# Cross-attention of a transformer block with keys on partitions, planned together with the end of self-attention

## Chip, cores and metric

The kernel runs on one core of a Trainium2 chip. The metric is device time in microseconds (us) of one launch. Five engines work side by side, each through its own list of instructions in program order: TensorE (PE, with weight loads shown apart as PEld), VectorE (DVE), ScalarE (ACT), GpSimd (POOL) and SyncE (SP, which here issues nearly all DMAs). They wait for each other through semaphores.

## What is computed

A transformer block over x of shape (2, 1024, 256): self-attention with 16 heads of 64, cross-attention to a context of 77 tokens, a gated feed-forward part with GELU, each behind a normalisation with shift and scale from a condition vector, and then a second feed-forward part with ternary weights and activations rounded to 8 bits. Cut to what matters here:

```python
h1 = adaln(x, t, norm1_w, norm1_b)
x = mha(h1, h1, attn1_wq, attn1_wk, attn1_wv, attn1_wo, attn1_bo) + x
h2 = adaln(x, t, norm2_w, norm2_b)
x = mha(h2, context, attn2_wq, attn2_wk, attn2_wv, attn2_wo, attn2_bo) + x
h3 = adaln(x, t, norm3_w, norm3_b)
x = glu_ff(h3, ff_w1, ff_b1, ff_w2, ff_b2) + x

def mha(xq, ctx, wq, wk, wv, wo, bo):        # 16 heads of 64
    q, k, v = xq @ wq, ctx @ wk, ctx @ wv
    attn = softmax(q @ k.T / sqrt(64))       # per head
    return (attn @ v) @ wo + bo
```

## The kernel before

The 2048 tokens are 16 tiles of 128, eight per batch element (`TB = 8`, `NT = 16`); the residual stream `r_sb` stays in SBUF throughout. All matmuls up to the ternary part are fp32.

**Self-attention** runs over 32 units (`NU`): batch element, pair of heads, half of the 1024 queries. Each unit has eight blocks of 128 keys, two per slot, so four slots per unit (`SLOTS`) and 128 in all (`NS`). Keys lie on partitions, queries in the free dimension. A slot issues the scores of its two key blocks (L351, into the two banks of `two_banks`), the copy out of PSUM on ACT (L970), the running maximum on DVE (L367), and, seven slots behind (`LAG`), the shift by the maximum (L404, DVE; one block of eight on POOL, L399), the exponential (L408, ACT), the running sum (L415, POOL) and the product with the values (L423). The maximum over all keys goes through a transpose and folds on DVE (L372 to L389), a small DMA to DRAM and a broadcast back (L390, L391); ACT then copies it to PSUM (L395). The sums are made by a matmul with ones (L455), go to DRAM and back in a packed form, are inverted on DVE (L486) and come back as a broadcast (L482 to L489) for POOL's multiplication (L499). Projections, values and the way back to tokens (`back_to_tokens`, its residual add L338) are spread over the slots by hand (`pieces`, `inner`, `extras`).

**The end of self-attention.** Slots 128 to 139 work off what the last units still have to do. The sums of the last two units are made by `sums_by_ones` (L444), for the last unit one matmul pair per key block, and inverted without packing by `inverted` (four reciprocals, L496). Six half tiles of cross-attention scores are laid between (`tail`), and the projection of the last four heads comes in one piece (`po_last`).

**Cross-attention, prepared.** During self-attention `CrossPair` forms for each pair of heads G = wq k^T and U = v wo of the 77 context tokens, so that scores are h G and the output is p U. They go to DRAM and are loaded whole (`load_g`, `load_u`).

**Cross-attention, before.** Queries lie on partitions. For each tile of 128 queries and each half of the heads: scores (`cross_scores`, L769: four groups of 308 columns, heads times 77 keys, over two halves of the 256 features), maximum per head and subtraction on DVE (L784, L787), exponential (L796, ACT), sum and reciprocal on DVE (L801, L802), division on POOL (L803). Then ten transposes of 128x128 (`cross_turned`, L815), copies (L823, L824, L826), ten output matmuls with U (`cross_out`, L836) and the residual add (L848). The loop `for n in range(3, NT + 1)` runs scores of tile n and output of tile n - 1 alternately; the norms for the next parts (L155, L162) and the ternary weights (L1104 to L1149) hang in it at slots given by hand (`mid`, `after`).

**After that** come the feed-forward part and the ternary part, ordered by a planner (`Plan`): steps with an engine, a cost, predecessors, a rank and possibly a ring of buffers; `Plan.run` issues them in the order in which a list schedule with these costs would start them. The order on each engine is fixed then; the costs have no other meaning. The up matmuls are L1611, the down matmuls L1637, the ternary matmuls L1466 and L1513, their transposes L1454 and L1502.

PSUM is full in both kernels: two pairs of banks by `two_banks` (tag "s"), one bank "f" (`piece_bank`), one bank "av", and one pair "mb".

The loop over tiles, cut:

```python
for n in range(3, NT + 1):
    cross_scores(n, 0); cross_shifted(n, 0)
    cross_turned(n - 1, 0)
    cross_exp(n, 0); cross_divided(n, 0)
    cross_scores(n, 1); cross_shifted(n, 1)
    cross_turned(n - 1, 1)
    cross_exp(n, 1)
    po = cross_out(n - 1)
    cross_divided(n, 1)
    cross_added(n - 1, po)
```

## Time and profile before

| | us |
|---|---|
| median of 3 runs | 1192.07 (1191.5 to 1193.33) |
| profiled execution | 1191.9 |
| its span, first to last instruction | 1190.1 |
| first cross-attention scores on PE | 766.4 |
| feed-forward matmuls without a break from | 969.65 |

Times in the profile count from the start of the span. A row of the groups gives the source line, engine, operation, output and inputs, count, busy time and mean duration of one in ns, and the idle time of the engine just before with what ended it. A row of the stretches gives start and end, length, and then for PE, PEld, DVE, ACT and POOL the busy time with the number of instructions that start in it, the clock granted to PE as a share of the full one, and the share and rate of the DMAs. Rows in order of time give start, duration, engine, line, operation, and in brackets an idle time with its releaser. Matmuls are pipelined, so their durations overlap; from start to start is their pace. Every fp32 matmul of the code shows as two records.

### The profile page before, as it was taken

The page shows a single profiled execution, that of the slowest core. Times are in us where ns is not written, and L with a number is a line of the kernel's source. Part 1 is how long each engine was busy: PE and PEld are TensorE (multiplying, and loading weights), DVE is VectorE, ACT ScalarE, POOL GpSimd, SP SyncE. Part 2 cuts the span into 40 slices and gives each one's busy share as a digit, 9 for nine tenths or more (in the row PEclk, how much of TensorE's full clock was granted, in tenths as well). Part 3 has the DMA queues.
Part 4 walks back from the last instruction along what each step waited for, and adds up shares of the span by engine and source line. Part 5 has one row for each costly group of instructions (what it writes and reads, how often), then busy time and mean ns, then how long its engine had stood idle before and what let it go on. Part 6 is the DMA issues. An engine that isn't in the chain of part 4 may idle for free.

```text
span 1190.1 us, 16832 instructions
## 1 busy us (share of the span) xinstructions
PE 1153.1 (97%) x5972; PEld 565.8 (48%) x5980; DVE 947.2 (80%) x1397; ACT 810.3 (68%) x1034; POOL 811.4 (68%) x628
## 2 busy tenths in 40 slices
PE   8998999999999999999999999999999999999996
PEld 4332334333334343343333332346878856486684
DVE  5798889789889888998888988984767753578596
ACT  4788887888887887888789788651343441555366
POOL 5689888888888888889888998941425325423244
PEclk9999999999999999999999999999999999999996
DMA  7011211222121221211213112210020021000000
GB/s 236 32 32 50 80 46 60 73 61 66 50 79 47 70 71 48 77 41 60 65 45 123 37 46 90 90 54 36 1 83 5 1 63 36 1 18 10 9 10 27
DMA packets 66013, 63.24 MB, mean 53 GB/s; under 512 B 22935, under 2 KB 56329, under 8 KB 65417
## 3 DMA queue, kind: packets, MB, share of 16 engines
q1 hardware_dynamic: 65865, 62.15, 16.9%
q8 instruction: 47, 0.77, 0.3%
q14 instruction: 37, 0.30, 0.1%
q10 hardware_dynamic: 64, 0.02, 0.0%
HBM read 54.63 MB, written 7.52 MB: 52 GB/s over the span
## 4 chain that ended last, share of the span: by engine, by line
PE 80%; DVE 11%; ACT 4%; issue 2%; DMA 1%; POOL 1%; ACTq 0%; DVEq 0%; POOLq 0%; SPq 0%
PE sc L351 17%; PE pav L423 16%; PE pu L1611 9%; PE pp L285 8%; PE sc L769 5%; PE po L836 5%; PE pv L285 4%; PE po L1637 4%; DVE macc L367 4%; DVE sT L404 3%; PE po L285 3%; ACT sT L970 2%; PE tot L455 1%; PE pu L1466 1%; PE po L1513 1%
## 5 line engine op out<-in xcount | busy, mean ns | idle before, releaser
L415 POOL TENSOR_TENSOR pacc<-pacc,sT 128x1024 f32<-128x1024 f32 x186 | 441.4, 2373 | 47.2 <-ACT sT L408 37.2
L970 ACT COPY sT<-sc 128x1024 f32<-128x1024 f32 x256 | 247.8, 1015 | 54.9 <-PE sc L351 45.7
L367 DVE TENSOR_TENSOR macc<-macc,sc 128x1024 f32<-128x1024 f32 x192 | 233.7, 1217 | 63.7 <-ACT sT L970 52.0
L408 ACT ACTIVATE sT<-sT 128x1024 f32<-128x1024 f32 x256 | 259.9, 1062 | 16.1 <-DVE sT L404 14.8
L351 PE MATMUL sc<-qT,kT 64*128 64x512 f32 x1024 | 258.0, 619 | 6.5 <-DVE macc L367 5.8
L404 DVE TENSOR_TENSOR sT<-sT,mb 128x1024 f32<-128x1024 f32 x225 | 261.7, 1207 | 3.0 <-ACT mb L395 3.0
L423 PE MATMUL pav<-sT,v 128*64 128x512 f32 x1024 | 250.1, 606 | 5.3 <-ACT sT L408 4.9
L351 PEld LDWEIGHTS sc<-qT,kT 64*128 64x128 f32 x1024 | 85.7, 185 | 146.1 <-DVE macc L367 63.9
L423 PEld LDWEIGHTS pav<-sT,v 128*64 128x64 f32 x1024 | 62.3, 136 | 155.6 <-issue 76.8
L1611 PE MATMUL pu<-h2T,ffw 128*128 128x512 f32 (+1 forms) x320 | 114.6, 509 | 0.0
L803 POOL TENSOR_TENSOR pr<-pr,t 128x616 f32<-128x616 f32 x32 | 38.9, 1217 | 104.1 <-DVE t L802 59.9
L415 POOL TENSOR_TENSOR pacc<-sT 128x1024 f32<-128x1024 f32 x31 | 73.9, 2384 | 36.9 <-ACT sT L408 36.9
L1611 PEld LDWEIGHTS pu<-h2T,ffw 128*128 128x128 f32 x320 | 59.5, 190 | 44.0 <-issue 39.9
L769 PE MATMUL sc<-G,h1T 128*128 128x308 f32 x256 | 73.2, 429 | 4.5 <-DVE pr L787 3.6
L836 PE MATMUL po<-U,pT 128*128 128x256 f32 (+1 forms) x320 | 72.8, 381 | 3.9 <-ACT pT L826 2.4
L399 POOL TENSOR_TENSOR sT<-sT,wide 128x1024 f32<-128x1024 f32 x31 | 73.7, 2378 | 1.6 <-DMA wide<-md 1.6
L836 PEld LDWEIGHTS po<-U,pT 128*128 128x128 f32 (+1 forms) x320 | 59.3, 190 | 13.0 <-ACT pT L826 3.2
L285 PE MATMUL pp<-h1T,wk 128*64 128x512 f32 x256 | 60.6, 594 | 0.9 <-ACT h1T L561 0.9
L285 PE MATMUL pv<-wv,h1T 128*64 128x256 f32 x512 | 60.8, 379 | 0.0
L285 PE MATMUL pp<-h1T,wq 128*64 128x512 f32 x256 | 60.5, 593 | 0.0
L1629 DVE SCALAR_TENSOR_TENSOR gT<-pu,vecT,ge 128x512 f32<-128x512 f32 (+1 forms) x40 | 25.6, 641 | 42.0 <-ACT ge L1622 41.7
L769 PEld LDWEIGHTS sc<-G,h1T 128*128 128x128 f32 x256 | 46.9, 191 | 23.2 <-issue 6.2
(190 smaller groups left out, 1518.5 us busy)
## 6 DMA issues: line engine op xcount, KB each, us to landing
wide<-md SPq DMA_DIRECT2D x32, 512.0 KB
rinv<-td SPq DMA_DIRECT2D x60, 128.0 KB
ffw<-in_L_xcond_ff_w_dram SPq DMA_DIRECT2D x3, 1024.0 KB
gd<-cw SPq DMA_DIRECT2D x32, 77.0 KB
ud<-cw SPq DMA_DIRECT2D x32, 77.0 KB
G<-gd SPq DMA_DIRECT2D x2, 1232.0 KB
wk<-in_L_xcond_attn_wk_dram SPq DMA_DIRECT2D x16, 128.0 KB
wq<-in_L_xcond_attn_wq_dram SPq DMA_DIRECT2D x16, 128.0 KB
```

Source lines behind the costliest of these rows:

```text
L285: nc.tensor.matmul(dst[half, :], lhsT=lhsT[:, half], rhs=rhs, start=start, stop=stop)
L351: nc.tensor.matmul(sc[:, j * 512 : (j + 1) * 512], lhsT=kTs[b, pair][rows, kb * P : (kb + 1) * P], rhs=qTs[b, pair][rows, qh * 512 : (qh + ...
L367: nc.vector.tensor_tensor(maccs[u], old, sc, ALU.max)
L399: nc.gpsimd.tensor_tensor(t, t, wides[u], ALU.subtract)
L404: nc.vector.tensor_tensor(sT[u, kb], sT[u, kb], mbs[u], ALU.subtract)
L408: nc.scalar.activation(t, t, AF.Exp)
L415: nc.gpsimd.tensor_tensor(paccs[u], old, t, ALU.add)
L423: nc.tensor.matmul(pavs[u][j * DH : (j + 1) * DH, :], lhsT=vs[b, pair // 2][:, kb, at : at + DH], rhs=sT[u, kb][:, j * 512 : (j + 1) * 512 ...
L769: nc.tensor.matmul(sc[:, i * 512 : i * 512 + HB * CTX], lhsT=hT[:, c, qb * P : (qb + 1) * P], rhs=Gs[b][:, c, at : at + HB * CTX], start=( ...
L836: nc.tensor.matmul(po[:, :D], lhsT=pT2s[n, part][:w, i * P : (i + 1) * P], rhs=Us[b][:w, half * 5 + c, :], start=(half + c == 0), stop=(ha ...
L970: nc.scalar.copy(sT[v, kb], sc)
L1611: nc.tensor.matmul(pu[:, k * 512 : k * 512 + n], lhsT=ffw1[c][:, at : at + P], rhs=hT[:, c, at0 : at0 + n], start=(c == 0), stop=(c == DC ...
```

## The change

Cross-attention is turned round: keys on partitions, queries in the free dimension, in batches of 512 queries (four batches). The 77 keys become 80 (`KEYS`, three of them doubled), so that 16 heads times 80 keys make ten pieces of 128 rows: piece i holds keys i, i + 10, ... of each head, eight per head. The doubled keys are taken out of the softmax by a bias of -30000 on the last row of each head (`again`) in the three last pieces. A batch has five tiles of two pieces (1024 columns). The maximum over keys is taken over all pieces on DVE, turned by four transposes, folded per head, spread and turned back; the sums are made on POOL and go the same way. The output needs no transposes any more: the quotients stand as PE wants them.

```diff
+        KP = P // H
+        NPIECE = -(-CTX // KP)
+        KEYS = KP * NPIECE
+        TWICE = KEYS - CTX
-        HK = H * CTX
+        HK = H * KEYS
...
+        def load_g(b):
...
+            Gs[b] = [t.rearrange("p (x i) -> p i x", i=NPIECE) for t in halves]
+        def load_u(b):
+            Us[b] = gu.tile([P, GU], FP, tag="gu", name="U").rearrange("p (i d) -> p i d", d=D)
+            nc.sync.dma_start(out=Us[b], in_=ud[b].rearrange("(p i) d -> p i d", i=NPIECE))
...
+        class Batch:
+            def scores(self, k):
+                sc = self.sc[k] = two_banks("sc2")
+                hT = norms[1, self.b].hT
+                for j in range(2):
+                    for c in range(DC):
+                        nc.tensor.matmul(
+                            sc[:, j * 512 : (j + 1) * 512],
+                            lhsT=Gs[self.b][c][:, 2 * k + j, :],
+                            rhs=hT[:, c, self.at : self.at + 512],
+                            start=(c == 0), stop=(c == DC - 1),
+                        )
+                self.t[k] = p3.tile([P, 1024], FP, tag="sT", name="p2")
+            def kept(self, k):
+                nc.scalar.copy(self.t[k], self.sc[k])
+            def larger(self, k):
...
+                nc.vector.tensor_tensor(self.macc, old, self.sc[k], ALU.max)
+            def largest(self):
+                m = self.macc[:, :512]
+                nc.vector.tensor_tensor(m, m, self.macc[:, 512:], ALU.max)
+            def turned(self, bank, src=None):
+                for i in range(4):
+                    at = slice(i * P, (i + 1) * P)
+                    nc.tensor.transpose(bank[:, at], src[:, at], ident)
+            def folded(self, op):
+                nc.vector.tensor_reduce(
+                    few, self.bank.rearrange("p (x k) -> p x k", k=KP), AX.X, op
+                )
+                if op == ALU.add:
+                    nc.vector.reciprocal(few, few)
...
+                nc.vector.tensor_copy(
+                    self.wide.rearrange("p (x k) -> p x k", k=KP),
+                    few.unsqueeze(2).to_broadcast([P, 4 * H, KP]),
+                )
+            def shifted(self, k):
+                nc.vector.tensor_tensor(t, t, self.both(self.bank), ALU.subtract)
+            def exponential(self, k):
+                if piece + 1 < DOUBLE:
+                    nc.scalar.activation(t, t, AF.Exp)
+                elif piece >= DOUBLE:
+                    nc.scalar.activation(t, t, AF.Exp, bias=again)
...
+            def running_sum(self, k):
+                nc.gpsimd.tensor_tensor(self.pacc, old, self.t[k], ALU.add)
+            def total(self):
+                nc.gpsimd.tensor_tensor(m, m, self.pacc[:, 512:], ALU.add)
+            def inverse_kept(self):
+                nc.scalar.copy(self.rinv, self.bank)
+            def divided(self, k):
+                if k < 2:
+                    nc.gpsimd.tensor_tensor(t, t, self.both(self.rinv), ALU.mult)
+                else:
+                    nc.vector.tensor_tensor(t, t, self.both(self.bank), ALU.mult)
+            def out(self, i, bank):
+                for piece in range(NPIECE):
+                    at = piece % 2 * 512 + i * P
+                    nc.tensor.matmul(
+                        po[:, :D],
+                        lhsT=self.t[piece // 2][:, at : at + P],
+                        rhs=Us[self.b][:, piece, :],
+                        start=(piece == 0), stop=(piece == NPIECE - 1),
+                    )
```

The twelve slots after the loop are gone, with `sums_by_ones`, `inverted` and the tail of scores. The loop ends at slot 127, and one plan orders everything from there to the end of cross-attention on PE, ACT, DVE, POOL and SP: what is left of the last three units, the last projection in four pieces, the norms, the four batches and the ternary weights. `Plan` moves ahead of self-attention for that and learns to take costs in two parts (busy, and until the result is there) and predecessors that count for order alone (`behind`).

```diff
-        for slot in range(NS + 12):
+        for slot in range(NS):
...
-        def sums_by_ones(tot, src, start, stop):
...
-        def inverted(u, part):
...
+        for u in (LAST - 2, LAST - 1, LAST):
+            s = add("PE", 0.75, lambda u=u: summed(u, piece_bank), [running.get(u)], -55, "f")
+            s = add("ACT", 0.37, lambda u=u: sums_kept(u), [s, normal.get(u - 1)], -55)
+            s = add("SP", (2.2, 4.9), lambda u=u: sums_packed(u), [s], -55)
+            s = add("DVE", 0.2, lambda u=u: inverted_packed(u), [s], -55)
+            s = add("SP", (4.2, 6.5), lambda u=u: inverted_spread(u), [s], -55)
+            normal[u] = add(
+                "POOL", 1.3, lambda u=u: normalised(u), [s, evac.get(u), normal.get(u - 1)], -55
+            )
...
+        plan.run({"s": 2, "f": 1, "av": 1, "A": 1, "B": 1})
```

The feed-forward weights (`load_ff`) are now loaded after the last scores instead of during self-attention, into the buffers that G of the second batch element had. Last, the plan of the feed-forward and ternary parts gets 22 steps whose results nobody reads, each of two bf16 matmuls of 256 columns, after the last piece and with the lowest rank:

```diff
+        def spare():
+            pd = two_banks("pd")
+            for f in range(2):
+                nc.tensor.matmul(
+                    pd[:, :D], lhsT=ident_bf, rhs=w2T[:, f, :], start=True, stop=True
+                )
+        for _ in range(22):
+            plan.add("PE", 0.36, spare, [piece.last], 99.0, "s")
```

On PE the order of the parts in the changed program, after the last self-attention scores, is: the last products with the values between the first eight score tiles; the last projection between the score tiles of batch 1; batch 2's scores and batch 0's outputs; batch 3's scores; then outputs of batches 1 to 3, with the transposes of the softmax, the norms and the ternary weights between them; then the feed-forward part in the order it had.

## The prediction, before the run

> **What bounds the kernel now.** I read the page first, then the groups with their shapes kept apart, then the stretches, then TensorE's (PE's) instructions in order of time from the end of self-attention to the feed-forward part.
>
> ```profile
> PE 1153.1 (97%) x5972; PEld 565.8 (48%) x5980; DVE 947.2 (80%) x1397; ACT 810.3 (68%) x1034; POOL 811.4 (68%) x628
> ...
> L769 PE MATMUL sc<-G,h1T 128*128 128x308 f32 x256 | 73.2, 429 | 4.5 <-DVE pr L787 3.6 <-DMA G<-gd 0.9
> ...
> L444 PE MATMUL tot_last<-sT,ones 128*64 128x512 f32 x32 | 8.4, 602 | 0.0
> ...
> L815 PE MATMUL pt_a<-ident,pr 128*128 128x128 f32 x128 | 16.7, 274 | 0.0
> ```
> ```profile
> 766.40:969.60 203.20, 194.66 (x974) 141.99 (x975) 146.44 (x261) 74.98 (x118) 78.20 (x89) 0.99 0.10 33
> 969.60:1163.20 193.60, 192.77 (x840) 129.29 (x846) 125.94 (x305) 93.02 (x137) 71.53 (x177) 1.00 0.07 22
> 1163.20:1190.10 26.90, 16.35 (x94) 10.04 (x93) 17.71 (x39) 17.34 (x22) 13.53 (x45) 0.66 0.09 30
> ```
> ```profile
> 774.72 3.13 PE L769 MATMUL sc<-G,h1T 128*128 128x308 f32 x8 [3.57 <-DVE pr L787]
> ...
> 836.90 2.24 PE L769 MATMUL sc<-G,h1T 128*128 128x308 f32 x8
> 838.97 1.04 PE L815 MATMUL pt_a<-ident,pr 128*128 128x128 f32 x8
> 839.85 2.24 PE L769 MATMUL sc<-G,h1T 128*128 128x308 f32 x8
> 841.92 0.38 PE L815 MATMUL pt_b<-ident,pr 128*104 128x128 f32 x2
> 842.14 4.49 PE L836 MATMUL po<-U,pT 128*128 128x256 f32 x20
> ...
> 969.65 10.52 PE L1611 MATMUL pu<-h2T,ffw 128*128 128x512 f32 x24
> ...
> 1169.61 3.59 PE L1466 MATMUL pu<-w1T,zT 128*128 128x512 bf16 x8 [1.52 <-ACT zT L1460]
> ```
>
> PE is the bound, and it is so in the very stretch that the change rewrites: between the first cross score (766.4) and the uninterrupted feed-forward part (969.65) it is busy 194.7 of 203.2 us, DVE 146, ACT 75, POOL 78 (columns two to five). So a microsecond of PE work removed there is one removed from the time, if no other chain comes up. The in-order rows give the pace, which is what counts, since single durations overlap: a tile of 128 queries starts at 836.90 and the next at 846.47: 9.57 us, made of two halves of scores (2.07 each to the next start), ten transposes (0.88 + 0.22) and the output (4.33). Every fp32 matmul of the code stands as two records. Only in the last 26.9 us does PE not bound; there the granted clock is 0.66.
>
> **The Trainium skill.** (1) "TensorE: Matmul & The Clock Gate", section "Step-by-step: what each phase is for": weight loads are pulled ahead of running matmuls while matmuls stay in program order. The trace agrees: the loads of L769 last 190 ns and its matmuls start every 260 ns. (2) The same page, "What's actually happening": after an idle window of about 3.4 us the clock is halved. The trace agrees: after 3.57 us of waiting at 774.72, eight records took 3.13 instead of 2.08 us, and in the tail eight bf16 records took 3.59. (3) "SBUF — State Buffer", in "Door 1: The DMA port swizzle", where it speaks of cachelines: reads at full rate need at least two hits in a line of 16 bytes, four fp32. No trace here has a strided weight load; it is the large unknown below.
>
> **The change, part by part.** First PE's work between 766.4 and the feed-forward part, before against after, at the paces of the rows:
> - Scores: 16 tiles x 2 x 2.08 = 66.6. After: 4 batches x 5 tile pairs x 4 matmuls of 512 columns = 160 records at 0.43 (24 records of L1611 in 10.3 us on the chain of waits) = 68.8.
> - Transposes: 160 of 128x128 at 0.11 = 17.6. After, 4 batches x 16 (largest, spread back, sum, spread back) = 64: 7.0.
> - Sums of the last two units of self-attention: 36 records of L444 at 0.215 (four in 0.86) plus one sum in quarters (0.5) = 8.2. After, three in quarters: 1.5.
> - Alike in both: the outputs 16 x 4.33 = 69.3 (ten matmuls a tile either way), 56 records of L423 at 0.234 = 13.1, the last projection 7.1, norms 3.5, ternary weights 2.1.
>
> Before: 66.6 + 17.6 + 8.2 + 95.1 = 187.5. The stretch lasted 203.3, of which six feed-forward records (2.6) are not its own: 200.7. So 13.2 us were lost, 8.5 as idle time and the rest as cold clock and uncovered starts. After: 68.8 + 7.0 + 1.5 + 95.1 = 172.4, or 15.1 less.
>
> Then what PE waits for in the new order, which I followed instruction by instruction on all engines from 766.4:
> - The sum of unit 29 now goes to the bank "f", which the residual add of the last projection empties. That add (L338) stood at 768.69; it now comes straight after the two maxima, which end at 767.64, and takes 0.66. PE waits from 766.4 to 768.4: 2.0.
> - The last maximum: three shifts (1.21 each) and the fold (3.7, from L372 at 769.29 to 772.99) end at 775.6. From the fold to the copy of the maximum took 7.25 us (772.99 to 780.24) with its two DMAs: 782.8; copy 1.0; then seven shifts hold DVE for 8.5 us, each with an exponential 1.06 behind it on ACT. The pairs of times_v are then ready at 788.3, 790.4 and 792.6. PE, with four score tiles (3.44 each) ahead of them, comes at 788.8: it loses about 0.9. The two maxima of batch 0 queued behind those shifts on DVE are late by 7 us, but hold only one of the two score banks, until 793.6, when PE needs it at 794.6.
> - Unit 31's sums: POOL's seven adds (2.37 each) run 788.3 to 804.9; then through SP two round trips by DRAM (4.7 and 7.0 in before) to POOL's multiply at about 822. The projection that needs it is reached by PE at 822.3: 0.7.
> - Batch 1's half of the norm: residual adds, statistics, POOL's root (14 small operations, 3 us, behind batch 0's four adds), four ACT instructions of 0.59, transposes, two of 0.78: the first score of batch 2 starts at about 831 instead of 829.4, with 0.9 lost before the transposes: 2.5 in all, less what the sums of batch 0 hide; I take 1.9.
> - From there PE has outputs (17.3 us a batch) to lay under every softmax chain. The last chain is longest: largest spread back, two shifts and exponentials (3.6), four adds and the halving on POOL (10.8), 15.4 with the ternary clip ahead on DVE; beneath it lie an output of batch 1, two of batch 2 and the ternary transposes, 13.9: 1.5 lost. Quotients before the next outputs: 0.3 twice.
> Sum: 2.0 + 0.9 + 0.7 + 1.9 + 1.5 + 0.6 = 7.6; I add 2.0 for uncovered starts, of which before had about 4.7. The other engines have room: of some 182 us DVE needs about 4 x 19.6 (twelve 1024-element passes of 1.2, two folds, adds) + 43 = 121, POOL 4 x 15.6 + 48 = 110. The last batch keeps two outputs of batch 2 for cover, so POOL's longer share does not take over.
>
> 172.4 + 9.6 = 182.0, against 200.7: 18.7 won.
>
> The edits with small answers: 80 keys instead of 77 in keys_values, g_heads and u_heads lengthen 192 short matmuls of self-attention by 4% of 300 ns, two at once: +0.3. The added ACT copies are hidden under PE. The six feed-forward records that ran early now run later: that is the 2.6. DMAs: feed-forward weights now load only after the last score, some 60 us before their use; G and U of batch element 1 land before batch 2 and its outputs. SP's row loads wait for the end of the stage as in before (969.98), and so does POOL's residual. The feed-forward part keeps its order on PE.
>
> **The spare matmuls** stand in PE's gaps after the last piece, two records of 256 columns in each of 22. Their gain is the clock: the eight records at 1169.61 would take 1.8, so the first bias add, which starts the rest of the chain, comes 0.9 earlier, and the last transposes and outputs gain 0.6: -1.5. Price if they stand in the way: five in a row are 1.2 us before a transposition; two such places cost 2.4. I take -1.5, and 0 to +1.5 for the range.
>
> Sum against the profiled execution: 766.4 + 0.3 + 182.0 = 948.7; the rest of before, 1190.1 - 969.65 = 220.4, plus 2.6, minus 1.5 = 221.5: span 1170.2. Around the span lay 1191.9 - 1190.1 = 1.8: 1172.0. The median of the runs lies 0.17 above the profiled execution: 1172.2.
>
> **The unknown: the strided weight load.** Batch.scores takes every tenth of 1280 columns as stationary operand, 40 bytes apart; before they were adjacent. Lower end: nothing, while a load stays under the 430 ns of the matmul that covers it, 2.26 times today's 190. Upper end, an estimate from the page on SBUF: adjacent weights share lines of four, so a load that pays per line takes 4 x 190 = 760 ns, and 160 records then cost 0.33 each: +53. It cannot gain, as the pace is the matmul's 430. I take nothing, since the margin is more than double.
>
> **Rivals.**
> - A, the forecast: PE stays the bound; 1172, own range 1165 to 1179.
> - B, waits in the fixed order: PE runs in program order, so every joint of PE, DVE and POOL (16 transposes of rows) that comes late stops all behind it. For it: POOL's seven plus four adds of 2.37 in sequence; against: outputs as cover. Two us more at the three last joints, and the early waits (5.5) doubled: +11.5, so 1183.5 (1179 to 1190).
> - C, slower: the strided load, at the 20 score tiles. It costs from 430 ns a load on; at 190 x 4 it ends at 1172 + 53 = 1225. The gain of 20 is gone at 430 + 20/160 = 555 ns.
> - D, nothing won: spare matmuls and late joints eat it all: about 1192. POOL with 110 of 182 us speaks against it.
>
> **How the numbers follow.** A 0.70, B 0.15, C 0.11, D 0.04. The range from 1163 to 1187 holds nearly all of A and most of B, eight in ten. About 0.2% (2.4 us) is what a measurement here can tell from none. Faster: A and B, 0.85; within it: most of D, 0.03; slower: C and the rest of D, 0.12.
>
> **What would show it.** Right: scores of 128x512 at 0.43 a record with loads near or under 430 ns; transposes of 64 instead of 160; no L444; PE busy over 95% between the last self-attention score and the feed-forward part, which starts near 949; granted clock near 1 in the tail. Wrong: loads of the scores longer than 430 ns (C); idle PE of more than 15 us before that start, with releasers DVE or POOL at the joints (B); a tail after the last feed-forward output longer than 27 us (spares in the way).

## The result, and the profile after

The changed kernel takes 1182.22 us (median of four, 1181.06 to 1184.35) where the kernel before takes 1192.45 beside it: a ratio of 0.9914, 95% interval 0.9902 to 0.9926. That is 10 us won where 20 were forecast. The profiled execution was the slowest of the four (1184.35, span 1181.7). Five more executions, beside later runs, had a median of 1179.42 (ratio 0.9899, 0.9881 to 0.9917), so medians of two kernels tell differences of some 3 us, not of one. The experiments below are therefore read mainly from the stretch of the profile that the change rewrites.

The stretches of the changed kernel, cut at the end of self-attention's last projection inside the slots, at the first uninterrupted feed-forward matmul and at 27 us before the end; the columns are as before:

```profile
768.33:960.72 192.39, 182.09 (x756) 130.50 (x757) 134.24 (x187) 80.79 (x101) 117.46 (x106) 0.98 0.12 40
960.72:1154.50 193.78, 193.33 (x828) 128.14 (x827) 125.10 (x299) 91.28 (x135) 71.22 (x177) 1.00 0.07 22
1154.50:1181.70 27.20, 18.91 (x163) 13.40 (x161) 19.83 (x46) 17.96 (x22) 13.50 (x45) 0.97 0.09 30
```

The whole deviation is in the first row: 192.4 us for a stretch that was forecast at 182.0, with GpSimd's busy time up from 78 to 117. From there to the end it is 221.0, forecast 221.5, and the clock of the tail is 0.97 instead of 0.66. In front of it the changed kernel is 2.1 us late from the first 17 us on, before self-attention's first score, and falls behind by another 0.35 up to 683 us, which I put down to the 80 keys (forecast 0.3). The 2.1 are not the change's: in the other profiles of this kernel and its variants below, that start lies between 0.1 earlier and 1.9 later than in the kernel before.

TensorE's instructions of the changed kernel in order of time, with what it waited for:

```profile
770.38 1.08 PE L522 MATMUL tot<-pacc,ones 128*32 128x256 f32 x8 [2.06 <-DVE r_sb L412]
771.39 3.11 PE L499 MATMUL pav<-sT,v 128*64 128x512 f32 x8
774.43 3.81 PE L846 MATMUL sc<-h1T,G 128*128 128x512 f32 x8
778.17 3.65 PE L499 MATMUL pav<-sT,v 128*64 128x512 f32 x16
...
894.05 3.81 PE L846 MATMUL sc<-h1T,G 128*128 128x512 f32 x8 [1.73 <-DVE macc L862]
...
930.57 1.60 PE L1407 MATMUL pt_w<-ident_bf,wq 128*128 128x128 bf16 x15 [2.91 <-DVE wq L1393]
...
932.81 5.18 PE L937 MATMUL po<-U,p 128*128 128x256 f32 x20
```

Three things are to be seen. The forecast wait for the residual add is there to the tenth (2.06). Two waits nobody had forecast stand at 894 and 930, both with VectorE as releaser. And behind the waits of 2.06 and 2.91 TensorE is slow for a while: the eight products with V take 3.04 from start to start instead of 1.87, twenty output records 5.0 instead of 4.33; the granted clock of 769.0 to 772.4 was 0.70, of 930 to 934 it was 0.60, and taken over 2 us it went down to 0.55 and to 0.50.

That slowness is not in every execution. The same kernel profiled again (c0 below) has the same waits, and no slow clock after them:

```profile
766.65:955.79 189.14, 178.84 (x757) 128.70 (x758) 134.33 (x187) 81.02 (x101) 117.53 (x105) 1.00 0.12 40
```
```profile
768.71 0.64 PE L522 MATMUL tot<-pacc,ones 128*32 128x256 f32 x8 [2.06 <-DVE r_sb L412]
...
927.28 1.01 PE L1407 MATMUL pt_w<-ident_bf,wq 128*128 128x128 bf16 x15 [2.90 <-DVE wq L1393]
928.57 4.48 PE L937 MATMUL po<-U,p 128*128 128x256 f32 x20
```

So 3.25 of the 10.4 us that the profiled execution was over the forecast stretch are slow clock, and 7.1 are there at full clock too. The spans of the two profiles differ by 5.3 us: 1.7 in front of the stretch, 3.25 in it and 0.4 behind it. From here on 189.1 is the stretch that the others are compared with, and where one had a slow clock I say so.

### The profile page after: what moved, and what is told of

It is laid out like the page before. It is cut to its first block, busy times and chain, and to the rows that moved or that the text cites. A ratio compares the mean times of both kernels' runs of the same rounds, so it can differ in the third digit from the quotient of the medians.

```text
span 1181.7 us, 16400 instructions
## 1 busy us (share of the span) xinstructions
PE 1146.3 (97%) x5812; PEld 557.9 (47%) x5812; DVE 936.0 (79%) x1324; ACT 814.7 (69%) x1017; POOL 849.5 (72%) x644
## 4 chain that ended last, share of the span: by engine, by line
PE 78%; DVE 14%; ACT 5%; issue 2%; DMA 1%; POOL 1%; SPq 0%; DVEq 0%; ACTq 0%; POOLq 0%
PE sc L425 17%; PE pav L499 16%; PE pp L360 8%; PE pu L1799 8%; PE sc L846 5%; PE pv L360 4%; PE po L1825 4%; DVE macc L441 4%; PE po L937 4%; DVE sT L481 3%; PE po L360 3%; ACT sT L1072 2%; PE tot L522 1%; PE pu L1654 1%; DVE p L896 1%
## 5 line engine op out<-in xcount | busy, mean ns | idle before, releaser
L491 POOL TENSOR_TENSOR pacc<-pacc,sT 128x1024 f32<-128x1024 f32 x192 | 455.6, 2373 | 47.2 <-ACT sT L484 36.7
L846 PE MATMUL sc<-h1T,G 128*128 128x512 f32 x160 | 74.1, 610 | 2.8 <-DVE macc L862 1.7
L937 PE MATMUL po<-U,p 128*128 128x256 f32 x320 | 71.6, 382 | 0.0
L937 PEld LDWEIGHTS po<-U,p 128*128 128x128 f32 x320 | 60.7, 192 | 8.3 <-issue 0.2
L360 PE MATMUL po<-wo,aT 128*64 128x256 f32 x512 | 61.1, 380 | 0.2 <-POOL aT L555 0.2
L846 PEld LDWEIGHTS sc<-h1T,G 128*128 128x128 f32 x160 | 47.2, 304 | 26.0 <-DVE macc L862 4.1
```

The costliest lines, as they stand in the source:

```text
L360: nc.tensor.matmul(dst[half, :], lhsT=lhsT[:, half], rhs=rhs, start=start, stop=stop)
L491: nc.gpsimd.tensor_tensor(paccs[u], old, sT[u, kb], ALU.add)
L846: nc.tensor.matmul(sc[:, j * 512 : (j + 1) * 512], lhsT=Gs[self.b][c][:, 2 * k + j, :], rhs=hT[:, c, self.at : self.at + 512], start=(c == 0),
L937: nc.tensor.matmul(po[:, :D], lhsT=self.t[piece // 2][:, at : at + P], rhs=Us[self.b][:, piece, :], start=(piece == 0), stop=(piece == NPI ...
```

## The experiments

My theory when I began: the missing gain comes from the strided weight load, part of which shows at each score tile, and from VectorE's ternary instructions, which are three times as long beside GpSimd and stand ahead of what TensorE waits for (theory 1). Rivals: heads of score tiles cost what they cost whatever the stride (2); the softmax chain of the last batch, with GpSimd in it, sets the end, so that a wait taken away only moves (3); the two waits have another cause (4).

The table gives for each kernel the stretch (less feed-forward records that stand in it), TensorE's idle time in it, and the ratio of the whole time to the kernel before, in order of the runs.

| run | stretch | idle | whole against before (95%) |
|---|---|---|---|
| changed kernel, first profile | 192.4 | 10.0 | 0.9914 (0.9902 to 0.9926) |
| e1_adjacent | 189.7 | 10.5 | 0.9876 (0.9861 to 0.9892) |
| e2_w2_late | 191.0 | 11.2 | 0.9917 (0.9903 to 0.9931) |
| e4_score_first | 188.2 | 9.1 | 0.9904 (0.9889 to 0.9920) |
| e5_no_clip | 187.1 | 6.7 | 0.9867 (0.9853 to 0.9881) |
| c0_after_again | 189.1 | 10.0 | 0.9899 (0.9881 to 0.9917) |
| e6_order_first | 189.0 | 9.8 | 0.9887 (0.9872 to 0.9902) |
| e7_costs | 189.4 | 8.7 | 0.9894 (0.9881 to 0.9908) |
| e8_act | 188.7 | 9.7 | 0.9884 (0.9865 to 0.9903) |
| e3_no_spares | 192.4 | 10.0 | 0.9916 (0.9900 to 0.9931) |
| e11_late_pool | 188.4 | 9.1 | 0.9883 (0.9867 to 0.9898) |
| e10_best | 181.0 | 3.9 | 0.9819 (0.9805 to 0.9832) |
| e12_scalar | 188.8 | 8.2 | 0.9879 (0.9861 to 0.9897) |

### The changed kernel again

> The changed kernel itself, beside the others of this call, for its spread: its executions differ by 3 us, and its profiled one was the slowest. If the slow clock behind the wait of 2.06 us at the start of the stretch is a matter of chance, as the run with the late second weight suggests (its sum took 0.64 us and its product with V 1.94 behind the same wait), this profile may have a stretch of about 190.8 us in place of 192.4. The time: 1182 +- 1.

Measured: 1179.42 us, stretch 189.1, as shown above; both are below what was expected, the stretch because the second slow clock is gone too and not only the first. Of the eight profiles that contain the wait of 2.06, four were slow behind it and four were not.

### The stride of the weight load

```diff
-            Gs[b] = [t.rearrange("p (x i) -> p i x", i=NPIECE) for t in halves]
+            Gs[b] = [t.rearrange("p (i x) -> p i x", i=NPIECE) for t in halves]
```

> Piece i takes 128 adjacent columns of G as its stationary operand in place of every tenth column. The order of all instructions is that of the changed kernel; a piece then holds whole heads and not eight keys of each head, so the maxima and sums are taken over other groups of scores and the output is another. Theory 1 (the stride makes the weight load longer, and the part of it that no matmul covers is paid at each score tile): the load of the cross-attention scores falls from 302 to about 190 ns, a score tile that stands alone from 3.74 to about 3.6 us, a record inside a group from 0.45 to 0.43, and the stretch between the end of self-attention and the feed-forward from 192.4 to between 188.5 and 190.2 us; the whole 2 to 4 us faster than the changed kernel, about 1179. Theory 2 (what stands at the head of a score tile is a cost of starting a group after other work, whatever the stride): the load falls all the same, but tiles stay at 3.74 and the time within 0.5 us. Theory 3 (the chain of batch 3's softmax sets the end of the stretch): tiles get shorter, the waits behind them longer, and the stretch stays above 191.5.

Measured: the loads fall to 190 ns. The weight loads of the scores, then a score tile and its successor on TensorE, first of the changed kernel, then of this one (minimum, median and maximum in ns; for the tiles start and duration):

```profile
L846 PEld LDWEIGHTS sc<-h1T,G x160: 299/302/327, 774.4 to 896.8; 128*128 128x128 f32 x160
```
```profile
818.53 3.81 PE L846 MATMUL sc<-h1T,G 128*128 128x512 f32 x8
822.27 1.95 PE L360 MATMUL po<-wo,aT 128*64 128x256 f32 x16
```
```profile
L846 PEld LDWEIGHTS sc<-h1T,G x160: 186/190/338, 771.4 to 893.2; 128*128 128x128 f32 x160
```
```profile
815.16 3.70 PE L846 MATMUL sc<-h1T,G 128*128 128x512 f32 x8
818.80 1.95 PE L360 MATMUL po<-wo,aT 128*64 128x256 f32 x16
```

From start to start the tile takes 3.74 with the stride and 3.64 without. Eight records at the forecast pace of 0.43 are 3.44; what is over is 0.30 in one case and 0.20 in the other, just the length of one weight load. So here one load of the tile, the first by this arithmetic, is covered by nothing; the others are. It is so wherever tiles start behind other work, and not at each tile: the 20 tiles stand in 14 groups, of which, in the changed kernel at full clock, eight are over by 0.3, five by 0 to 0.2, and the last, four tiles with the wait of 1.73 between them, by 0.9. Theory 1 is right in the mechanism, but its size is wrong: the scores fall from 72.8 to 71.8, and to 71.3 without the slow clock in the first tile (4.13 from start to start where the next takes 3.63): by 1.5 and not by 2 to 4. Two thirds of the cost of a group's head are there without the stride, which is theory 2's part. The stretch of 189.7 contains this slow clock behind the first wait (1.2 more in the products with V, 13.8 us in all instead of 12.6) and longer waits (10.5 for 10.0). At full clock it would be about 188.1: of the 1.5 saved in the scores, 0.5 went into new waiting.

### The second ternary weight later

```diff
-            s = add("PE", 1.1, lambda name=name: ternary_turned(name), last, 45, "s")
+            s = add("PE", 1.1, lambda name=name: ternary_turned(name), last, 45 if name == "w1" else 95, "s")
```

> The transposes of the second ternary weight go behind the softmax of batch 3 (rank 95 for 45), so that TensorE doesn't wait for the clip and the rounding on VectorE ahead of batch 3's sums. Theory 1 (the wait of 2.91 us and the cold clock behind it are a loss of their own): the stretch falls by 3 to 4.5 us, from 192.4 to 188 to 189.5. Theory 3 (GpSimd's sums end at 929.96 and the join, the fold, the second join, the copy and the quotients follow them, some 12 us, whatever TensorE does before): the next tile of outputs takes the place of the wait, the join of the sums still starts at about 932.0, and the first outputs of batch 3 at about 943 where they were at 943.6: the stretch falls by 0.3 to 1.5 us only. I hold theory 3 the likelier for this run.

Measured: 191.0, so 1.9 longer than the changed kernel at full clock. TensorE of this kernel, in order of time:

```profile
926.97 4.58 PE L937 MATMUL po<-U,p 128*128 128x256 f32 x20 [1.62 <-DVE r_sb L949]
...
939.87 1.13 PE L937 MATMUL po<-U,p 128*128 128x256 f32 x4 [1.36 <-POOL p L928]
942.19 3.07 PE L937 MATMUL po<-U,p 128*128 128x256 f32 x13 [1.18 <-POOL p L928]
```

The 2.9 us are gone and 4.16 have come in their place; the outputs, now broken into more runs, take 0.6 more besides, at full clock. The output tile that moved forward waits for a bank whose residual add stands on VectorE behind the same ternary clip, and at the end TensorE waits twice for GpSimd's quotients. Theory 3 holds, more strongly than I had expected: moving the waiting instruction leaves its cause where it was.

### The first score tile first

```diff
-                score[n, k] = add("PE", 3.5, lambda x=x, k=k: x.scores(k), waits, r, "s", room)
+                score[n, k] = add("PE", 3.5, lambda x=x, k=k: x.scores(k), waits, r if j else -60, "s", room)
```

> The first score tile of batch 0 is issued ahead of the sum of unit 29 (rank -60 for 0), whose bank isn't free before the residual addition. Theory 1 (the wait of 2.06 us and the slow clock behind it are paid in full): no idle TensorE at the start of the stretch, the sum takes 0.5 us instead of 1.0, the first product with V 1.9 instead of 3.0, and the stretch falls by 3 to 3.8 us, from 192.4 to about 189. Theory 3 (later chains set the end): the gain is met by longer waits before 800 us or at the end, and the stretch falls by less than 1 us.

Measured, TensorE in order of time:

```profile
766.64 3.81 PE L846 MATMUL sc<-h1T,G 128*128 128x512 f32 x8
770.38 0.64 PE L522 MATMUL tot<-pacc,ones 128*32 128x256 f32 x8
...
781.25 0.64 PE L522 MATMUL tot<-pacc,ones 128*32 128x256 f32 x8 [1.19 <-POOL pacc L491]
```

The 2.06 are gone, and 1.19 come back eleven us later, where the sum of unit 30 now stands before GpSimd has finished its additions. Against 189.1 the gain is 0.9. Theory 3's bound (less than 1 us) is met; against the first profile it would have looked like 4.2.

### VectorE without the clips

```diff
         def ternary_clip(name, i, low):
-            t = raws[name][i]
-            if low:
-                nc.vector.tensor_scalar(t, t, -1.0, MAGIC, ALU.max, ALU.add)
-            else:
-                nc.vector.tensor_scalar(t, t, parts8[name], 1.0, ALU.mult, ALU.min)
+            return
```

> The scaling and clipping of the ternary weights is left out (eight VectorE instructions, L1388 and L1390; the rounding stays), so that the ternary weights are wrong; the order of all other instructions is that of the changed kernel. Theory 1 (the two waits that I had not forecast come from these instructions, which stand ahead of the maxima and of the rounding on VectorE and run at a third of their pace beside GpSimd): the 1.73 us before batch 3's fifth score tile go, the 2.91 us before the second ternary weight's transposes go, what is left is about 1.4 us of waiting for GpSimd's total, and the stretch falls by 3.5 to 5 us. Theory 3 (GpSimd sets the pace): the first wait goes, the second is replaced by one for the total, and the stretch falls by 1.7 to 2.5 us. Theory 4 (the waits have another cause, a late buffer or a transfer): both stay.

In the changed kernel VectorE and GpSimd show the cause of the wait at 894. VectorE, in order of time, and then GpSimd:

```profile
876.39 0.66 DVE L1388 TENSOR_SCALAR raw<-raw 128x1024 f32<-128x1024 f32 x1
...
888.37 1.73 DVE L1388 TENSOR_SCALAR raw<-raw 128x1024 f32<-128x1024 f32 x1
890.13 2.73 DVE L1393 TENSOR_SCALAR wq<-raw 128x1024 bf16<-128x1024 f32 x1
892.79 2.53 DVE L862 TENSOR_TENSOR macc<-macc,sc 128x1024 f32<-128x1024 f32 x2
```
```profile
884.73 7.58 POOL L912 TENSOR_TENSOR pacc<-pacc,p 128x1024 f32<-128x1024 f32 x3
```

The same clip takes 0.66 us while GpSimd rests and 1.73 while it adds; the maxima behind it, which read PSUM, take 1.19 to 1.22 each throughout. The Trainium skill has this in "SBUF — State Buffer", section "Who interferes with whom": VectorE's tensor_scalar from SBUF to SBUF can take a second port that it shares with GpSimd, one of the two blocks for the other's whole instruction, and an instruction with at most one SBUF input outside those modes is not touched. The traces agree as far as they go: in all profiles, those of the ternary instructions of 128x1024 that ran beside an idle GpSimd took 0.75 us at most, and a GpSimd addition that starts while one of them runs takes 2.68 instead of 2.37. No run moves GpSimd's work alone.

Without the clips the wait at 894 is gone, so is the one at 930, and 1.20 remain for GpSimd's total; idle time falls from 10.0 to 6.7. The stretch is 187.1 with a slow clock behind the first wait (products with V 13.9 instead of 12.6, sums 2.05 instead of 1.70: 1.7 us), so about 185.4 without it: 3.7 less than 189.1, within theory 1's 3.5 to 5. Theory 4 falls.

### Two gains together, and three that missed

The next three kernels share two edits: the early score tile of before, and pieces of G that lie side by side and are still eight keys of every head.

```diff
-                nc.scalar.copy(
-                    self.g.rearrange("p (j x) -> p j x", j=2),
-                    pg.rearrange("p (j x) -> p j x", j=2)[:, :, : DC * KB],
-                )
+                gv = self.g.rearrange("p (x i j k) -> p x i j k", x=DC * B, i=NPIECE, j=2)
+                for j in range(2):
+                    nc.scalar.copy(
+                        gv[:, :, :, j, :],
+                        pg[:, j * 512 : j * 512 + DC * KB].rearrange(
+                            "p (x k i) -> p x i k", x=DC * B, i=NPIECE),
+                    )
...
+                for b in range(B):
+                    for c in range(DC):
+                        nc.sync.dma_start(out=gd[b][:, c, :, at], in_=gv[:, c, b, :, :])
```

> The pieces of G lie as 128 adjacent columns, each still eight keys of every head: the copy that empties the heads' scores reorders them, and the transfers to DRAM write runs of 64 bytes instead of 320. The first score tile of batch 0 is issued ahead of the sum of unit 29. If both gains are separate (2.65 us and 3 to 4 us of the stretch in their runs), the stretch takes 185 to 187 us and the whole about 1176.5; if the softmax chain of batch 3 sets the end, the stretch stays above 188. The shorter runs to DRAM lie in self-attention, whose time stays within 0.5 us.

Measured: 189.0, a miss. The scores fall to 71.4, but the early tile brings 1.39 of waiting at 781, the waits of 1.83 and 2.91 stay, and the clock was slow behind the last one (about 1.6 us). Without that the stretch would be about 187.4, which is 1.7 less than the changed kernel at full clock, where the two edits alone came to 1.0 and 0.9: they do add up, and the expectation had read the parts (2.65 and 3 to 4) against a profile with slow clock. Self-attention is about 0.3 longer with the shorter runs to DRAM, which lies within the differences between the other runs.

The second tells the plan longer costs:

```diff
-                u = add("DVE", 1.27, lambda name=name, i=i: ternary_clip(name, i, False), [s], 80)
+                u = add("DVE", 2.8, lambda name=name, i=i: ternary_clip(name, i, False), [s], 80)
```

and so for the other clip and the rounding.

> As the run before, and the plan is told 2.8 us for each clip and rounding of the ternary weights in place of 1.27, 1.17 and 0.95, which is what they take beside GpSimd's additions. Theory 1 (the two waits come from a plan that took these steps for short ones): VectorE gets the maxima of batch 3 ahead of them, TensorE's waits for the fifth score tile and for the second ternary weight shrink by 2 us or more in sum, and the stretch is 1 to 3 us shorter than with the plan's old costs. Theory 3 (GpSimd's chain): no shorter by more than 0.5 us.

Measured: 189.4. The wait at the fifth score tile falls from 1.83 to 0.46 and the one before the second weight goes, but 2.53 us for GpSimd's quotients come in, and a slow clock behind them (outputs 71.4 us instead of 69.5); the early tile's wait at 784 is 2.03, with a slow clock too (scores 72.5 instead of 71.4). Theory 1's two waits did shrink as expected, by 4.3 us, but 3.2 of that came back as waits for GpSimd, which is theory 3's part: the idle time falls by 1.1, from 9.8 to 8.7.

The third moves the scaling to ScalarE:

```diff
-                nc.vector.tensor_scalar(t, t, -1.0, MAGIC, ALU.max, ALU.add)
+                nc.vector.tensor_scalar(t, t, MAGIC - 1.0, MAGIC + 1.0, ALU.max, ALU.min)
             else:
-                nc.vector.tensor_scalar(t, t, parts8[name], 1.0, ALU.mult, ALU.min)
+                nc.scalar.activation(t, t, AF.Copy, scale=parts8[name], bias=MAGIC)
```

> As the run with the ordered pieces and the early score tile, and the scaling of the ternary weights goes to ScalarE (times the inverse scale plus the rounding constant, in one activation), so that VectorE has two instructions for each half of a weight instead of three. Theory 1: the waits behind VectorE shrink, since a third of the slow instructions is gone; stretch 1 to 2.5 us shorter than without. Rival: ScalarE's copies and exponentials of the softmax come 1 us later for each of them, and nothing is won.

Measured: 188.7. One rounding was still on VectorE ahead of the maxima, took 2.84 us and made TensorE wait 1.95, with a slow clock behind it (granted 0.61 and 0.54 between 887 and 891, scores 72.7 instead of 71.4); behind the softmax 1.39 and 1.18 went to GpSimd's quotients.

### The spare matmuls

```diff
-        for _ in range(22):
+        for _ in range(0):
```

> The 22 spare steps behind the last piece are left out (their product is read by nobody). Theory 1 (they keep the clock up in the last 27 us, where TensorE waits for short chains of the other engines): the granted clock of the tail falls from 0.97 to about 0.66, the part behind the start of the feed-forward gets 1.5 to 2.5 us longer (from 221 to about 223), and so does the whole. Rival (what they give in clock they take by standing in front of the transposes): the tail keeps its length within 0.5 us though the clock falls.

The last 28.7 us of this kernel, from the same place in the work:

```profile
1154.00:1182.70 28.70, 17.19 (x119) 11.01 (x118) 19.85 (x46) 18.01 (x22) 13.76 (x46) 0.82 0.09 29
```

From the start of the feed-forward part to the end it takes 222.3 where the changed kernel takes 221.0 and 220.6 in its two profiles: the spare matmuls are worth 1.3 to 1.7 us. In the ten other variants this part takes 220.6 to 220.9, feed-forward records that ran ahead of it counted in, so the difference is clear of the scatter. The stretch before it (192.4) has the slow clock behind both waits, as in the first profile. The clock of the tail falls, to 0.82 and not to 0.66.

### The quotients of GpSimd

```diff
-                return k < 2
+                return k > 2
```

together with the late second weight.

> As the run with the late second ternary weight, and GpSimd takes the last two of the five quotients of a batch (k > 2) in place of the first two, so that TensorE, which reads them in order, meets GpSimd's at the end of a tile of outputs. If theory 3 is right (after the transposes are out of the way the end of the softmax chain, GpSimd's quotients, is what TensorE waits for), the waits of 1.36 and 1.18 us for GpSimd go, and the stretch falls from 191.0 to 188 to 189; 1.62 for the bank of an output stays. If the quotients' place doesn't matter: 191.

Measured: 188.4, and the waits of 1.36 and 1.18 for GpSimd have become one of 0.23; the 1.62 stays. The place of the quotients in the order in which TensorE reads them was what made it wait.

### All of it

Besides the ordered pieces, the early score tile, `k > 2` and the scaling on ScalarE, the last rounding goes to ScalarE, and the plan is told that unit 30's last addition is ready later:

```diff
-            nc.vector.tensor_scalar(
-                wqs8[name][:, i * 1024 : (i + 1) * 1024], raws[name][i], MAGIC, None,
-                ALU.subtract,
-            )
+            nc.scalar.activation(
+                wqs8[name][:, i * 1024 : (i + 1) * 1024], raws[name][i], AF.Copy, bias=-MAGIC,
+            )
...
-                    "POOL", 2.38, lambda u=u, kb=kb: running_sum(u, kb),
+                    "POOL", (2.38, 4.6) if (u, kb) == (LAST - 1, TB - 1) else 2.38, lambda u=u, kb=kb: running_sum(u, kb),
```

> Put together: ordered pieces, the early score tile with the sum of unit 30 a tile later, the last two quotients on GpSimd, and ScalarE takes the scaling and the last rounding step of the ternary weights, so that VectorE has one instruction for each half of a weight where it had three. Theory 1 (VectorE's slow instructions beside GpSimd made the two large waits) and theory 3 (then GpSimd's quotients) together: no wait over 1 us is left, idle TensorE in the stretch falls from 10 to 4 to 6 us, the stretch from 189.1 (undisturbed) to 183.5 to 186, the whole to about 1174. Rival (each wait taken away lets the next one grow, as in the runs before): idle stays at 8 us or more and the stretch above 187.5.

The stretch and TensorE's part at its end (lines are shifted by two or three in this kernel: L940 is the output, L876 the joins, L1801 the feed-forward):

```profile
768.61:951.29 182.68, 178.44 (x760) 111.90 (x761) 121.54 (x179) 88.51 (x109) 115.48 (x106) 1.00 0.13 42
```
```profile
926.03 0.60 PE L876 MATMUL join<-ident,pacc 128*128 128x128 f32 x4
926.47 4.48 PE L940 MATMUL po<-U,p 128*128 128x256 f32 x20
930.78 0.60 PE L876 MATMUL join<-ident,wide 128*128 128x128 f32 x4
931.22 1.04 PE L163 MATMUL pt_n<-ident,xn 128*128 128x128 f32 x8
932.09 1.88 PE L1801 MATMUL pu<-h2T,ffw 128*128 128x512 f32 x4
933.81 17.64 PE L940 MATMUL po<-U,p 128*128 128x256 f32 x80
```

No row here waits. The whole takes 1171.56 us (1170.6 to 1172.62), ratio 0.9819 (0.9805 to 0.9832): faster than both kernels. The stretch of 182.7 contains 1.7 of feed-forward; the rest, 181.0, is 8.1 less than the changed kernel at full clock: 6.0 idle time, 1.9 scores, 0.2 others. One at a time, at full clock, the parts had given 1.0 (adjacent pieces: 1.5 in the scores less 0.5 of new waiting), 0.9 (the early tile) and 0.7 (GpSimd's quotients with the late second weight); VectorE's relief alone gives about 2 without its slow clock (0.3 with it), as the last run shows. That is 4.7 in sum, so some 3.4 us come only when they stand together.

### VectorE's relief alone

The two edits that move ternary work to ScalarE, on the changed kernel.

> The changed kernel with one part of the best version alone: ScalarE takes the scaling and the last rounding step of the ternary weights, VectorE keeps one instruction for each half. Theory 1 alone (VectorE's steps are the whole of it): the waits of 1.73 and 2.9 us go and nothing takes their place, so the stretch falls by 4 us or more, to 185 or less in an undisturbed execution. Theory 1 with theory 3 (then the quotients of GpSimd are waited for): both waits go, and 1.5 to 2.6 us for GpSimd's quotients come in before batch 3's outputs; the stretch without the feed-forward records that stand in it is 186.5 to 188. The wait of 2.06 us at the start stays.

Measured: 188.8. The waits of 1.73 and 2.9 are gone, and those for GpSimd's quotients are there, on TensorE:

```profile
936.33 1.13 PE L937 MATMUL po<-U,p 128*128 128x256 f32 x4 [1.39 <-POOL p L928]
938.64 18.36 PE L937 MATMUL po<-U,p 128*128 128x256 f32 x76 [1.18 <-POOL p L928]
```

76 records at 0.2165 are 16.5; here they take 18.2 from start to start, a slow clock again. The outputs take 2.1 us more in all than in the changed kernel at full clock; without that the stretch would be about 187, where theories 1 and 3 together had it. Theory 1 alone (185 or less) doesn't hold.

## Why the prediction was off, step by step

The forecast went the right way, and 1182.2 lies in its range, but outside the own range of its likeliest case (1165 to 1179) and inside that of rival B, waits in the fixed order. Of the 7.1 us that are missing at full clock, 4.7 are TensorE's own work and 2.4 are waiting. Term by term, in the second profile of the changed kernel (time of each kind from the start of a row to the start of the next, less idle time):

| | forecast | measured |
|---|---|---|
| scores | 68.8 | 72.8 |
| transposes of rows | 7.0 | 7.6 |
| sums | 1.5 | 1.7 |
| outputs | 69.3 | 69.5 |
| products with V | 13.1 | 12.6 |
| last projection | 7.1 | 7.9 |
| norms | 3.5 | 4.8 |
| ternary weights | 2.1 | 2.3 |
| uncovered starts | 2.0 | in the rows above |
| waits | 7.6 | 10.0 |
| sum | 182.0 | 189.1 |

- **"160 records at 0.43 (...) = 68.8"** is the term that was mis-sized most, by 4.0. The pace came from 24 feed-forward matmuls in a row; the 20 score tiles stand in 14 groups between other work, and more than half of these show a whole weight load. The allowance of 2.0 for uncovered starts was a lump that met half of it. The stride costs 1.5 of the 4.0. Rival C's mechanism is real (302 ns for 190), its size was far off: 1.6 times, not four, and below the 430 from which it would have decided.
- **"15.4 with the ternary clip ahead on DVE"** took the clip at its pace beside a resting GpSimd. **"beneath it lie an output of batch 1, two of batch 2 and the ternary transposes, 13.9"** counted as cover an instruction that was itself the one to wait, for 2.9. VectorE was busy for 134 us in the stretch and not for 121. The page on SBUF that the prediction cites for the stride has the sharing of ports in a later section; with GpSimd's work reckoned to rise from 78 to 110 us it bore on this change.
- **The waits one by one**: the first, forecast 2.0, was 2.06; the products of unit 31 lost nothing instead of 0.9, its projection 0.2 instead of 0.7, batch 1's norm half 1.6 instead of 1.9 with 1.5 more at the two joins near it, the last chain and the quotients nothing, at their own places, instead of 1.5 and 0.6. 1.73 and 2.90 for VectorE had not been in the list. Errors of both signs are in the sum of 10.0 for 7.6.
- **No slow clock was counted behind 2.06 us of waiting**, though the prediction counted one behind 3.57 in the kernel before. In the first profile it cost 3.25 behind two waits.
- **Right**: outputs at 4.33, 64 transposes, no L444, the part behind the stretch (221.0 for 221.5), the spare matmuls (-1.5; 1.3 to 1.7), loads under 430 ns. TensorE is busy 94.6% of the stretch, a little under the 95 named, and idle for 10 and not the 15 us that would have meant rival B.
- **Right by luck**: 0.3 for the 80 keys (0.35). The factors named, 192 matmuls, 4% and 300 ns, give 2.3 us, or 1.2 if two run at once. From start to start these matmuls took 69 and 78 ns in the kernel before, not 300, and 71 and 80 in the changed one: 0.4 in all.
- **"if no other chain comes up"** was the condition on which a microsecond of TensorE work is one of time. The runs show that it doesn't hold: adjacent pieces took 1.5 us off TensorE's work, and the waits grew by 0.5; with the late second weight, the longer costs and VectorE's relief alone, waits of 2.5 us for GpSimd's quotients came in place of those removed. Only when the parts of the chain were eased together did the idle time fall to 3.9.

What stays open: why the same wait leaves the clock high in one execution and low in the next, and what makes the first 17 us of some executions 1.4 to 2.1 us longer. That GpSimd makes VectorE's instructions long rests on their durations; the runs show only that these instructions, once long, were what TensorE waited for.

## What to carry to other kernels

A pace read from a long run of matmuls holds inside a run; count each place where a group starts between other work at up to one more weight load. A step that you count as cover must itself be ready: look on its engine for what stands ahead of it, and beside which GpSimd work that runs, since VectorE's tensor_scalar from SBUF to SBUF lasted up to nearly four times as long there. When one wait is taken away, ask at once which chain ends next; here single edits gave 0.7 to 2 us of the stretch each at full clock, 4.7 in sum, and together 8. Before comparing two profiles, look for a slow clock in either: one such stretch cost 1.3 to 1.9 us here, more than most of the edits gave.

## What the runs showed of the hardware

- A weight load of 128x128 fp32 takes 302 ns from columns 40 bytes apart, 190 ns from adjacent ones (160 loads each).
- In the changed kernel a ternary tensor_scalar of 128x1024 on VectorE takes 0.66 to 0.75 us alone and 1.4 to 2.9 beside GpSimd's additions and quotients; a GpSimd addition that starts while one of them runs takes 2.68 instead of 2.37. The maxima, tensor_tensor with an operand in PSUM, keep their 1.2.
- The clock granted to TensorE fell to about 0.5, taken over 2 us, behind idle times of 1.95 to 2.91 us in some executions, and stayed at 1.00 behind waits of 2.06 and 2.90 in another of the same kernel. Behind two waits of 1.39 and 1.18, a microsecond apart, it fell in one kernel and not in two others with nearly the same waits. The Trainium skill, "TensorE: Matmul & The Clock Gate", section "What's actually happening", speaks of an idle window of about 3.4 us, which runs freely. The chance from one execution to the next fits that; that less than 3.4 us of idleness was enough is what the traces show beyond it.
- With transfers of 64-byte runs to DRAM, 98 thousand packets in all where there were 65 thousand, self-attention was 0.3 to 0.7 us longer in four kernels. Kernels without them differ among themselves by 0.9.
